# Four graph layers on one core: the block buffers lent to layer 3's first two column pairs, and six small copies moved from GpSimd to ScalarE

## The chip, the core and the metric

The kernel runs on one core of a Trainium2 chip. Its engines are TensorE (matmul; PE in the profile, PEld for its weight loads), VectorE (DVE), ScalarE (ACT), GpSimd (POOL) and SyncE (SP), which here only issues DMAs. The time is that of the device for one execution, in microseconds, from the slowest (here the only) core.

## The reference, cut to what matters

Four layers share one weighted adjacency matrix of 2708 x 2708 and node features of 2708 x 256. Every layer ends in `x = layernorm(x + layer(x))`.

```
# layer 0: adj @ (x * W)
# layer 1: masked attention of four heads, softmax over adj > 0
# layer 2: edge_output = GRU(adj' @ h, h);  edge_support = mean over 3 heads of
#              softmax(leaky(e) where adj' != 0) * adj' @ (h @ W_k)
#          node_output = GRU(edge_support, h)
#          diag(adj) * edge_output + diag(adj) * node_output     (adj' has no diagonal)
# layer 3: z = [x, (adj @ (x @ neigh_W.T)) / (adj.sum(1) + 1)] @ lin_W.T
```

The change lies in layer 2's node GRU and attention and in the start of layer 3's adjacency product.

## The kernel before, in words

The nodes are 22 row tiles of 128 (`NT`), the last with 20 rows. The adjacency comes from the host transposed and cut into 128 x 128 tiles (`adj_t`).

**Products by column pairs.** In layers 2 and 3 the adjacency product is done in seven block products in the place of eight (`seven`, L309): two adjacent column tiles of the matrix, `2c` and `2c+1`, and two row ranges, one from each half of the nodes, make a two by two block. `MH` is 11 such column pairs. VectorE forms sums and differences of the four quarters (L315 to L318), and TensorE does seven products at L328 into four accumulators (`m1`, `m26`, `m75`, `m43`). `gathered` (L332) empties these after the last pair: ScalarE copies `m1`, VectorE combines the rest at L339, L342, L345 and L346.

**Layer 2's attention** is a loop over three row ranges `units` of 512, 512 and 330 rows from each half, three heads `k`, and 11 column pairs `c` (L1336 to L1366). For each pair SyncE loads a block of the adjacency (`load_blocks`, L1147, through `load_pairs`, L259, with its DMAs at L275), and GpSimd clears the diagonal in it (`clear_own`, L278, operation at L286). ScalarE makes a tile `p` of exponentials (L1347, L1350), VectorE multiplies it by the block (L1351), and `seven` follows. The blocks go through three places: two buffers with the tag `blk` in the pool `hold`, and the end of the tile `turn`, in the order block, turn, block. The tiles `p` have three buffers in the pool `nright`. A load into a buffer waits until everything that used the tile before it is done.

**The node cells.** After a row range's heads, its GRU and the rows that follow are a generator, `node` (L1285), which is put into the list `later`; projections of a head go into `urgent` (L300). `between` (L302) takes one step of them; `seven` calls it after chosen products, so that the cells' matmuls stand between those of the next attention range, or of layer 3. Each half of a range goes through `cell` (L1193: gates at L1206, ScalarE at L1208 and L1211, VectorE at L1221 to L1227), then VectorE multiplies by the diagonal and adds the edge part (L1305, L1306), which gives `yt`, the rows transposed. `by_tiles` (L1268) cuts `yt` into the row tiles: a tile that lies whole in the range is used as it stands; of one that is cut by the end of the range, the part is copied into a tile of its own (L1278), and it is used when the second part has come. `node_rows` (L1234) then turns a tile back (TensorE at L1239, through the single PSUM buffer `bank`; ScalarE copies it out at L1241) and takes its moments (VectorE L171 to L175, GpSimd L176); `rows_end` (L1244) multiplies by the layer-3 weights (L1249), and ScalarE writes `h3`, layer 3's right-hand side, in `turn` (L1250), and the rest of the row, which GpSimd stores to memory (L1252). GpSimd also issues the loads for the cells (`load_cell`, L257; `load_diag`, L1265).

Of the row ranges, six partial tiles come from the node cells: two parts in the second half of range 0, two in the second half of range 1, one in each half of range 2. A part has 54 or 74 rows, and the copy moves 2 x 54 or 2 x 74 elements of each partition.

**Layer 3** (L1417 to L1435) has three row ranges `units3` of 430, 430 and 366 rows from each half and again the 11 column pairs, taken in the order `lead`: pairs whose rows of `h3` are ready early come first, so that layer 3 starts while range 2's node cells are still being worked off between its products (`early3`: a step after every product). Each pair is loaded into a tile `p` of `nright`, the same three buffers as in the attention. At the third-last pair of a range a tile `o8` with the tag `blk` is taken, and GpSimd loads into it the stored rows (L1431), which `rows3` (L1402) later adds to. `rows3` uses `by_tiles` as well.

**Order.** Each engine and each queue runs its instructions in a fixed order. It is set before the run by the programming framework, which starts from the order of the code and estimates when each instruction could run; an instruction can so be put ahead of one that stands before it in the code. `issue_after` keeps an instruction behind a named one on its engine: layer 3's pairs but the first are kept behind the end of `gathered` (L1432).

Of the kernel before, what the change touches and what calls it, by code (L numbers as in the profile page):

```python
# [9 lines left out]
F32 = mybir.dt.float32  # L10
# [9 lines left out]
P = 128  # L20
# [7 lines left out]
def kernel(  # L28
# [24 lines left out]
    nc = tc.nc  # L53
    N, F = x.shape
    NT = -(-N // P)
# [6 lines left out]
    W = GT * P  # L62
# [21 lines left out]
    tiles3 = [t for t in range(NT) if t not in last3]  # L84
    NH3 = (N - P * len(last3)) // 2
# [4 lines left out]
    def sz(i):  # L90
        return min(P, N - i * P)

    def width(lo, hi):
        return min(hi * P, N) - lo * P
# [4 lines left out]
    def pieces(lo, w, tiles=range(NT)):  # L99

        for t in tiles:
            a, b = max(lo, 0), min(lo + w, sz(t))
            if a < b:
                yield t, a, b
            lo -= sz(t)
# [5 lines left out]
    def pool(name, bufs=1, **kw):  # L111
        return tc.tile_pool(name=name, bufs=bufs, reuse_waits="tile", **kw)
# [287 lines left out]
    if True:  # L400
# [12 lines left out]
        if True:  # L413
# [39 lines left out]
            with pool("l0", 2) as l0:  # L453
# [49 lines left out]
                with pool("prep", side="right") as prep:  # L503
# [39 lines left out]
                    for f in range(FC):  # L543
                        for s in range(2):
# [7 lines left out]
                            at = s * (H + F)  # L552
# [50 lines left out]
                    t = ahead + 1  # L603
# [35 lines left out]
                t = NT - 1  # L639
# [25 lines left out]
            if True:  # L665
# [124 lines left out]
                for g in range(0, len(spans), 2):  # L790
                    segs = spans[g : g + 2]
                    at, w = segs[0][0] * P, width(segs[0][0], segs[-1][1])
# [20 lines left out]
                    for q in range(H // 2):  # L813
# [23 lines left out]
                        for b, c0 in enumerate(range(0, NT, 2)):  # L837
                            block = {}
                            for c in range(c0, min(c0 + 2, NT)):
                                block[c] = []  # L840
                                for i in range(2):
                                    p = next(held)
# [17 lines left out]
                        got = []  # L860
# [4 lines left out]
                        for s, (p0, ws) in enumerate(cols):  # L865
                            two = slice(2 * (s ^ q) * CT, 2 * ((s ^ q) + 1) * CT)
                            for i, (a, n) in enumerate(halves_at):
                                lo, hi = max(p0, a), min(p0 + ws, a + n)
# [42 lines left out]
                for t in range(NT):  # L911
                    for b, acc in zip(banks, pus):
                        w = width(*spans[b[0]])
                        for j, g in enumerate(b):
                            at = spans[g][0] * P
# [80 lines left out]
                for g in range(0, len(spans), 2):  # L996
                    two, w = range(g, g + 2), width(*spans[g])
                    acc = ps_t.tile([P, 4, P], F32, tag="tr", name="pq").rearrange("p i q -> p (i q)")
                    for t in range(NT):
                        for j, gg in enumerate(two):  # L1000
                            at = spans[gg][0] * P
# [36 lines left out]
                for lo in range(0, NT, 4):  # L1038
                    hi = min(lo + 4, NT)
                    at, w = lo * P, width(lo, hi)  # L1040
                    pt = ps_t.tile([P, 4, P], F32, tag="tr", name="pst")
                    for t in range(lo, hi):
                        n = sz(t)
# [5 lines left out]
                    for u, (a, uw_) in enumerate(units):  # L1049
                        for h in range(2):  # L1050
                            c0, c1 = max(at, h * NH + a), min(at + w, h * NH + a + uw_)
# [52 lines left out]
    hold = hold_stack.enter_context(pool("hold", side="right"))  # L1104
    with pool("e_work") as ework, pool("ps_g", 4, space=PSUM, side="right") as ps_g:
        wih, whh = weights(ework, "wih", e_wih), weights(ework, "whh", e_whh)
        for r, (a, w) in enumerate(raws):
            while len(edges) < min(r + 2, len(raws)):
                next(ahead)
            if r not in left:  # L1110
# [3 lines left out]
                yt = ework.tile([P, FC, 2 * w], F32, tag="yt", name="yt")  # L1114
# [9 lines left out]
    with (  # L1124
# [107 lines left out]
        shared, shared3 = {}, {}  # L1232

        def node_rows(t, src):  # L1234

            n = sz(t)
            pt = bank()
            for f in range(FC):
                nc.tensor.transpose(pt[:n, f * P : (f + 1) * P], src[:, f, :n], ident)  # L1239
            y = nleft.tile([P, F], F32, tag="y", name="y", bufs=3)  # L1240
            nc.scalar.copy(y[:n], pt[:n, :F])  # L1241
            return t, src, y, moments(y, n)[1]

        def rows_end(t, src, y, rs):  # L1244

            n = sz(t)
            pz = bank()
            for f in range(FC):
                nc.tensor.matmul(pz[:n], src[:, f, :n], lwn[:, f, :], start=(f == 0), stop=(f == FC - 1))  # L1249
            nc.scalar.activation(h3[t][:n], pz[:n, F:], AF.Copy, scale=rs)  # L1250
            nc.scalar.activation(y[:n], pz[:n, :F], AF.Copy, scale=rs)
            nc.gpsimd.dma_start(y3_d[t], y[:n])  # L1252

        def load_cell(lo, w):
            got = []
            for parts, tag in ((xt_d, "xt2"), (edge_d.values(), "et")):
                got.append(nleft.tile([P, FC, W], F32, tag=tag, name=tag))
                load_columns(got[-1], parts, lo, w, nc.gpsimd)
            return got

        def load_diag(lo, w):

            dst = nleft.tile([P, W], F32, tag="drow", name="drow")
            src = bass.AP(tensor=diag_d.tensor, offset=diag_d.offset + lo, ap=[[0, P], [1, w]])
            nc.gpsimd.dma_start(dst[:, :w], src)  # L1265
            return dst

        def by_tiles(lo, w, src, ends, among=range(NT)):  # L1268

            tiles, at = [], 0  # L1270
            for t, c0, c1 in pieces(lo, w, among):
                got = src(at, c1 - c0)
                at += c1 - c0
                if c1 - c0 < sz(t):
                    first = t not in ends
                    if first:
                        ends[t] = nleft.tile([P, FC, P], F32, tag=f"yt{len(ends)}", name=f"yt{t}")
                    nc.gpsimd.tensor_copy(ends[t][:, :, c0:c1], got)  # L1278
                    if first:
                        continue  # L1280
                    got = ends[t]
                tiles.append((t, got))
            return tiles

        def node(u, est):  # L1285

            a, w = units[u]
            nxt = None
            for h in range(2):
                lo = h * NH + a  # L1290
                xt, et = nxt or load_cell(lo, w)
                drow = load_diag(lo, w)
                yt = nleft.tile([P, FC, W], F32, tag="yt", name="yt")
                parts = [[a[:, j, :w] for j in range(FC)] for a in (xt, et, yt)]

                def prepare(j):

                    xj, ej, _ = (a[j] for a in parts)
                    nc.vector.tensor_tensor(ej, ej, drow[:, :w], ALU.mult)
                    nc.vector.tensor_tensor(ej, ej, xj, ALU.add)  # L1300

                def rest(j):

                    _, ej, yj = (a[j] for a in parts)
                    nc.vector.tensor_tensor(yj, yj, drow[:, :w], ALU.mult)  # L1305
                    nc.vector.tensor_tensor(yj, yj, ej, ALU.add)  # L1306

                yield from cell(est[h], xt, yt, w, *node_w, b_node, prepare, rest)
                yield
                tiles = by_tiles(lo, w, lambda at, n: yt[:, :, at : at + n], shared)  # L1310
                got = []
                for i in range(len(tiles) + 1):
                    if i < len(tiles):
                        got.append(node_rows(*tiles[i]))
                        yield
                    if i:
                        rows_end(*got[i - 1])
                        yield
                    if i == 1 and h == 0:
                        nxt = load_cell(NH + a, w)  # L1320
# [15 lines left out]
        for u, (_, w) in enumerate(units):  # L1336
            est = [nleft.tile([P, FC, W], F32, tag="est", name="est", bufs=3) for h in range(2)]
            for k in range(K):
                m = accumulators()
                for c in range(MH):  # L1340
                    blk = load_blocks(u, c)
                    pa = nright.tile([P, 2, 2, W], F32, tag="p", name="p", bufs=3)
                    for i in range(2):
                        p = pa[:, i]
                        at = 2 * c + i
# [16 lines left out]
                y, summed = gathered(nleft, m, w, W, "yk")  # L1362
# [6 lines left out]
        def complete(u):  # L1369

            return [t for t in tiles3 if ends3[t] == u]
# [25 lines left out]
        def room():  # L1397

            tag = next(free)
            return bank() if tag is None else ps_a.tile([P, 2, W], F32, tag=tag, name=tag)[:, 0]  # L1400

        def rows3(u, y, o8):  # L1402

            a, w = units3[u]
            for h in range(2):
                for t, src in by_tiles(h * NH3 + a, w, lambda at, n: y[:, :, h, at : at + n], shared3, tiles3):
                    pt = room()
                    for f in range(FC):
                        nc.tensor.transpose(pt[: sz(t), f * P : (f + 1) * P], src[:, f, : sz(t)], ident)
                    row3(t, o8[:, complete(u).index(t)], pt)  # L1410
                    yield
            flush()
# [4 lines left out]
        for u, (_, w) in enumerate(units3):  # L1417
            m = accumulators()
            for i, c in enumerate(lead):
                early3 = u == 0 and max(ends_at[2 * c], ends_at[2 * c + 1]) + 1 < len(units)  # L1420
                if u == 0:
                    if not early3:
                        while urgent or later:
                            between()
                    hq[c] = quarter_sums(xqp, h3, c, "hq")
                pa = nright.tile([P, 2, 2, W], F32, tag="p", name="p", bufs=3)
                load_pairs(units3, u, c, pa, NH3, tiles3)
                if i == MH - 3:
                    o8 = hold.tile([P, 4 * W // F, F], F32, tag="blk", name="o8", bufs=2)
                    for j, t in enumerate(complete(u)):  # L1430
                        nc.gpsimd.dma_start(o8[: sz(t), j], y3_d[t])  # L1431
                with tc.issue_after(summed.ins) if i else nullcontext():  # L1432
                    seven(nright, m, pa, h3, hq[c], c, w, i == 0, i == MH - 1, range(7) if early3 else (2, 5))
            y, summed = gathered(nleft, m, w, W, "yk")
            later.append(rows3(u, y, o8))  # L1435
# [287 lines left out]
```

## Time and profile before

| | |
|---|---|
| median of 3 runs | 1851.02 us (1850.7 to 1851.26) |
| the profiled execution's own time | 1851.49 us |
| its span, first to last instruction | 1849.7 us |
| mean granted TensorE clock | 0.996 |
| TensorE busy | 1822.9 us (99%) |
| VectorE busy | 1267.4 us (69%) |
| ScalarE busy | 698.7 us (38%) |
| GpSimd busy | 297.1 us (16%) |
| attention and node cells, about | 725 to 1600 us |
| layer 3, about | 1600 us to the end |

The profile is one execution. In its views, each line of a timeline gives start and length in us, the engine, the line of the kernel, the operation, what is written and read, how many instructions, and in brackets the idle time before them with what ended it. A tile is named with what it was allocated as; `m` are the accumulators, `bank` the single buffer of the cells, `hq` and `turn` layer 3's right-hand sides and sums of them, `xq` and `x` those of layer 2. One float product at L328 shows as two matmul records. A busy share of TensorE is not its speed: the granted clock beside it says how fast it ran.

### The profile page before, as it was taken

The numbers are of one execution on the slowest core, as the hardware profiler recorded it, in microseconds if no ns is written. First come the engines' busy times: TensorE is split into PE (matmuls) and PEld (weight loads), VectorE is DVE, ScalarE is ACT, GpSimd is POOL, SyncE is SP. The second block draws the span as 40 slices with busy tenths as digits, with TensorE's granted clock in tenths as the row PEclk, the third lists the DMA queues.
The fourth block names the chain that finished last, engine by engine and source line by source line (L and its number), as shares of the span: only waits on it lengthen the run. The fifth ranks groups of instructions, "written<-read, shape, count | busy, mean of one in ns | idle before, by whom it ended". The sixth has DMA issues, their size and how long they took to land.

```text
span 1849.7 us, 23045 instructions
## 1 busy us (share of the span) xinstructions
PE 1822.9 (99%) x7512; PEld 1039.6 (56%) x7512; DVE 1267.4 (69%) x2242; ACT 698.7 (38%) x1443; POOL 297.1 (16%) x447
## 2 busy tenths in 40 slices
PE   9999999999999999999999999999999999999997
PEld 7888843233456886887444444444445556554555
DVE  5333489998797655654658887777887767844664
ACT  3444420033245113111555665555664655321011
POOL 1332211011013410000011101211200302111211
PEclk9999999999999999999999999999999999999999
DMA  9343310000003657764557665454554545634774
GB/s 301 122 161 125 126 55 24 24 1 27 27 7 89 145 143 193 175 144 117 171 145 203 179 174 153 132 158 121 164 153 112 144 103 131 170 89 120 205 175 125
DMA packets 435711, 237.34 MB, mean 128 GB/s; under 512 B 184459, under 2 KB 422444, under 8 KB 433148
## 3 DMA queue, kind: packets, MB, share of 16 engines
q1 hardware_dynamic: 423534, 210.76, 42.1%
q0 software_dynamic: 7696, 20.50, 3.5%
q10 hardware_dynamic: 4350, 4.50, 0.7%
q8 instruction: 62, 1.02, 0.2%
q14 instruction: 69, 0.57, 0.1%
HBM read 223.00 MB, written 12.66 MB: 127 GB/s over the span
## 4 chain that ended last, share of the span: by engine, by line
PE 92%; DMA 3%; DVE 2%; SPq 1%; ACT 1%; issue 1%; POOL 0%; POOLq 0%; DVEq 0%
PE m L328 43%; PE acc L820 11%; PE acc L214 8%; PE bank L1206 7%; PE den L830 6%; PE gate L1081 4%; PE bank L1182 3%; PE bank L1249 2%; PE acc L519 2%; SPq L275 1%; PE pm L425 1%; PE m L1450 1%; DMA strip<-in_adj_t_dram 1%; PE pq L1002 1%; ACT below L472 1%
## 5 line engine op out<-in xcount | busy, mean ns | idle before, releaser
L844 DVE SCALAR_TENSOR_TENSOR p<-fall_b,rise,mask 128x1024 f32<-128x1024 f32 (+1 forms) x264 | 288.7, 1158 | 28.8 <-PE den L830 17.8
L1347 ACT ACTIVATE p<-st,e_neg 128x1024 f32<-128x1024 f32 (+1 forms) x198 | 197.6, 1042 | 195.1 <-PE m L328 190.0
L328 PE MATMUL m<-s,xq 128*128 128x512 f32 (+3 forms) x660 | 230.7, 468 | 0.0
L820 PE MATMUL acc<-p,h 128*64 128x512 f32 (+2 forms) x1056 | 210.5, 549 | 0.0
L315 DVE TENSOR_TENSOR s<-p 128x512 f32<-128x512 f32 (+3 forms) x132 | 81.9, 620 | 153.0 <-PE m L328 106.2
L328 PE MATMUL m<-p,xq 128*128 128x512 f32 (+1 forms) x396 | 183.5, 545 | 0.1
L214 PE MATMUL acc<-turn,strip 128*128 128x257 f32 x792 | 182.6, 381 | 0.3 <-DMA strip<-in_adj_t_dram 0.2
L1350 ACT ACTIVATE p<-p 128x1024 f32<-128x1024 f32 (+1 forms) x198 | 179.0, 944 | 0.2
L328 PE MATMUL m<-p,x 128*128 128x512 f32 (+1 forms) x396 | 167.6, 542 | 0.3 <-DVE supt L345 0.3
L328 PEld LDWEIGHTS m<-s,xq 128*128 128x128 f32 x660 | 124.7, 190 | 76.1 <-issue 59.0
L1351 DVE TENSOR_TENSOR p<-p,blk 128x1024 f32<-128x1024 f32 (+1 forms) x132 | 143.6, 1108 | 34.5 <-ACT p L1350 25.1
L214 PEld LDWEIGHTS acc<-turn,strip 128*128 128x128 f32 x792 | 147.2, 189 | 22.0 <-DMA strip<-in_adj_t_dram 1.4
L820 PEld LDWEIGHTS acc<-p,h 128*64 128x64 f32 x1056 | 72.7, 138 | 129.7 <-issue 122.2
L328 PE MATMUL m<-s,x 128*128 128x512 f32 (+3 forms) x330 | 127.2, 467 | 0.0
L328 PEld LDWEIGHTS m<-p,xq 128*128 128x128 f32 x396 | 74.9, 191 | 77.2 <-issue 61.9
L328 PEld LDWEIGHTS m<-p,x 128*128 128x128 f32 x396 | 74.8, 190 | 75.5 <-issue 60.9
L457 DVE TENSOR_SCALAR mask<-strip 128x2816 fp8e4<-128x2816 f32 (+5 forms) x40 | 39.3, 1012 | 109.2 <-DMA strip<-in_adj_t_dram 109.2
L830 PE MATMUL den<-p,h 128*32 128x512 f32 (+2 forms) x1056 | 110.5, 546 | 0.0
L286 POOL TENSOR_TENSOR blk<-blk,offdiag 128x128 f32<-128x128 f32 (+3 forms) x50 | 33.8, 681 | 365.4 <-DMA blk<-in_adj_t_dram 312.2
L472 ACT ACTIVATE below<-strip 128x384 bf16<-128x384 f32 x132 | 78.6, 595 | 18.3 <-DMA strip<-in_adj_t_dram 14.8
L328 PEld LDWEIGHTS m<-s,x 128*128 128x128 f32 x330 | 62.2, 191 | 39.0 <-issue 34.8
L316 DVE TENSOR_TENSOR p<-p 128x512 f32<-128x512 f32 (+3 forms) x132 | 81.6, 618 | 2.4
(286 smaller groups left out, 2652.6 us busy)
## 6 DMA issues: line engine op xcount, KB each, us to landing
strip<-in_adj_t_dram SPq DMA_DIRECT2D x19, 1408.0 KB, 6.0
blk<-in_adj_t_dram SPq DMA_DIRECT2D x88, 256.0 KB, 3.5
blk<-in_adj_t_dram SPq DMA_DIRECT2D x88, 192.0 KB, 4.1
pa<-in_adj_t_dram SPq DMA_DIRECT2D x110, 128.0 KB, 2.7
turn<-in_adj_t_dram SPq DMA_DIRECT2D x44, 256.0 KB, 3.1
blk<-in_adj_t_dram SPq DMA_DIRECT2D x88, 128.0 KB, 2.6
p<-in_adj_t_dram SPq DMA_DIRECT2D x88, 128.0 KB, 2.8
turn<-in_adj_t_dram SPq DMA_DIRECT2D x44, 192.0 KB, 3.2
```

The lines of the kernel that those rows point to most:

```text
L214: at = nc.tensor.matmul(acc, s[:, c, :n], rhs(c), start=(c == 0), stop=(c == NT - 1))
L315: nc.vector.tensor_tensor(s1, a21, a22, ALU.add)
L316: nc.vector.tensor_tensor(a21, a21, a11, ALU.subtract)
L328: nc.tensor.matmul(dst[:, :w], lt, rt, start=start and not (one_bank and i in (3, 4, 6)), stop=stop and not (one_bank and i in (1, 2, 5)))
L472: nc.scalar.activation(below[:, : (hi - lo) * P], s[:, lo:hi].rearrange("p c n -> p (c n)"), AF.Relu, scale=-1.0, accum_out=negative[:, BE ...
L820: at = nc.tensor.matmul(acc[s][i * HD : (i + 1) * HD, :ws], hs[c][:, 2 * q + i, :HD], ps[i][:, p0 : p0 + ws], **flags,)
L830: at = nc.tensor.matmul(den[j : j + CT, :ws], hs[c][:, 2 * q + i, HD + 1 - CT :], ps[i][:, p0 : p0 + ws], **flags,)
L844: nc.vector.scalar_tensor_tensor(p[:, :w], fall_b[:, i, :w], rise[:, c, 2 * q + i : 2 * q + i + 1], mask[:, c, at : at + w], ALU.max, ALU. ...
L1206: nc.tensor.matmul(g[:, :w], lt, rt, start=(q == 0), stop=(q == len(terms) - 1))
L1347: nc.scalar.activation(p[:, :, :w], st_k[:, :, :w], AF.Relu, scale=-1.0, bias=e_neg[:, at, k : k + 1])
L1350: nc.scalar.activation(p[:, :, :w], p[:, :, :w], AF.Exp, scale=-1.0)
L1351: nc.vector.tensor_tensor(p[:, :, :w], p[:, :, :w], blk[:, i, :, :w], ALU.mult)
```

## The change

It has two parts that don't depend on each other.

`by_tiles` takes the copying instruction as a parameter. The node cells pass ScalarE's copy, layer 3's `rows3` passes GpSimd's, which it was for both. In layer 3, for the first row range's first two pairs, the tile is taken from the two `blk` buffers of `hold`, under the name `p3`, and not from the three `p` buffers of `nright`; the third pair is then the first in a `p` buffer. The size of these tiles is the same, so the memory in use stays what it was. `o8` takes the same two buffers after them.

```diff
-        def by_tiles(lo, w, src, ends, among=range(NT)):
+        def by_tiles(lo, w, src, ends, copy, among=range(NT)):
...
-                    nc.gpsimd.tensor_copy(ends[t][:, :, c0:c1], got)
+                    copy(ends[t][:, :, c0:c1], got)
...
-                tiles = by_tiles(lo, w, lambda at, n: yt[:, :, at : at + n], shared)
+                tiles = by_tiles(lo, w, lambda at, n: yt[:, :, at : at + n], shared, nc.scalar.copy)
...
-                for t, src in by_tiles(h * NH3 + a, w, lambda at, n: y[:, :, h, at : at + n], shared3, tiles3):
+                for t, src in by_tiles(h * NH3 + a, w, lambda at, n: y[:, :, h, at : at + n], shared3, nc.gpsimd.tensor_copy, tiles3):
...
-                pa = nright.tile([P, 2, 2, W], F32, tag="p", name="p", bufs=3)
+                if u == 0 and i < 2:
+                    pa = hold.tile([P, 2, 2, W], F32, tag="blk", name="p3", bufs=2)
+                else:
+                    pa = nright.tile([P, 2, 2, W], F32, tag="p", name="p", bufs=3)
                 load_pairs(units3, u, c, pa, NH3, tiles3)
                 if i == MH - 3:
                     o8 = hold.tile([P, 4 * W // F, F], F32, tag="blk", name="o8", bufs=2)
```

## The prediction

> **What bounds the kernel now.** First the page's chain of work that ended last:
>
> ```profile
> PE 92%; DMA 3%; DVE 2%; SPq 1%; ACT 1%; issue 1%; POOL 0%; POOLq 0%; DVEq 0%
> ```
>
> TensorE is the chain, so only a stretch in which TensorE stands still, or runs slowly, can be won. The waits of TensorE alone, from 1200 us to the end (the last third, where the change lies; columns: total, times, longest), name them:
>
> ```profile
> PE m L328 <- DVE yk L339: 2.6, 1, 2.6
> PE bank L1239 <- POOL yt L1278: 2.5, 2, 2.2
> PE bank L1409 <- POOL yt L1278: 0.2, 1, 0.2
> ```
>
> That is all: two real stalls in 650 us. One is at L1278, the copy that moves to ScalarE; the other is where layer 3 begins. The windows show what each costs beyond its idle time (columns: stretch, length, PE, PEld, DVE, ACT and POOL busy, granted clock, DMA share, GB/s):
>
> ```profile
> 1526.00:1534.00 8.00, 5.78 (x18) 3.66 (x17) 4.73 (x11) 3.36 (x7) 4.48 (x8) 0.79 0.39 100
> 1552.00:1600.00 48.00, 48.00 (x174) 32.47 (x174) 46.11 (x102) 28.09 (x41) 9.89 (x19) 1.00 0.57 143
> 1600.00:1606.00 6.00, 4.46 (x16) 2.62 (x14) 1.45 (x3) 0.44 (x1) 0.53 (x1) 1.00 1.11 299
> 1606.00:1612.50 6.50, 5.41 (x11) 2.63 (x12) 6.36 (x11) 0.00 (x0) 0.00 (x0) 0.74 0.61 149
> ```
>
> Between the stalls TensorE is full at clock 1.00; just after each the clock is 0.79 and 0.74.
>
> Stall A, in order of time, GpSimd first, then TensorE:
>
> ```profile
> 1527.22 1.48 POOL L286 TENSOR_TENSOR blk<-blk,offdiag 128x128 f32<-128x128 f32 x2 [4.84 <-DMA blk<-in_adj_t_dram]
> 1528.65 0.58 POOL L1265 DMA_DIRECT2D drow<-diag_d  x1
> 1529.24 0.53 POOL L1278 COPY yt<-yt 128x108 f32<-128x108 f32 x2
> ...
> 1529.57 0.69 PE L1239 MATMUL bank<-ident,yt 128*128 128x128 f32 x2 [2.22 <-POOL yt L1278]
> 1530.06 1.31 PE L328 MATMUL m<-s,xq 128*128 128x330 f32 x2
> ```
>
> The copy's input was ready at 1526.83 (VectorE's L1306: 1526.14 + 0.69). The copy ran at 1529.24 because GpSimd's queue held the diagonal clearing of an adjacency block (L286), which waited 4.84 us for its load, and a load of the diagonal (L1265). All engines then stood: VectorE waited 2.08 us at L171, ScalarE 2.81 at L1241.
>
> Stall B, SyncE's queue, VectorE, TensorE:
>
> ```profile
> 1586.38 2.00 SPq L275 DMA_DIRECT2D blk<-in_adj_t_dram  x4
> 1595.44 4.79 SPq L275 DMA_DIRECT2D p<-in_adj_t_dram  x9
> ...
> 1604.52 0.61 DVE L315 TENSOR_TENSOR s<-p 128x430 f32<-128x430 f32 x1 [5.47 <-DMA p<-in_adj_t_dram]
> ...
> 1606.20 0.84 DVE L339 TENSOR_TENSOR yk<-m1s,m 128x660 f32<-128x660 f32 x1
> ...
> 1607.09 0.99 PE L328 MATMUL m<-p,turn 128*128 128x430 f32 x2 [2.63 <-DVE yk L339]
> ```
>
> SyncE had nothing to do from 1588.38 to 1595.44: layer 3's first pair needs a "p" buffer, free only when TensorE has read the third-last attention block. Its seven loads land near 1604.3. VectorE holds that pair's L315 to L317 ahead of L339, which empties the accumulators of the attention; TensorE's second product of layer 3 wants those accumulators. So a late load stops TensorE through VectorE's order.
>
> **What the Trainium skill says.** "TensorE: Matmul & The Clock Gate", section "What's actually happening": after about 3.4 us of idleness the array runs at half clock and needs about as long a busy time to return. The trace agrees in kind: idle 2.22 and 2.63 us, then two products of 330 columns take 1.31 us instead of 0.72. The same page, "Architectural detail": ScalarE's, VectorE's and GpSimd's queues are strictly in order; L1278 standing behind L286 agrees. "ScalarE: Activation LUTs", "What ACT_TABLE_LOAD costs": 186 ns + 0.833 ns an element without pointer operands, so an estimated 276 ns for 108 elements and 309 for 148. The trace's nearest row, L336 copying 226 elements, takes 349 ns (formula: 374), so it holds to 7%. "DMA: Bandwidth & Descriptors", "Issuing engines are not separate DMA queues": loads issued by GpSimd and by SyncE share the 16 engines. Agrees: with eleven "o" loads of 128 KB from GpSimd between 1588.6 and 1600, the first pair's loads saw a DMA share of 1.11 and its seventh took 5.8 us to land (all L275 loads: median 2.8).
>
> **The change, part by part.**
>
> *Copies.* Six leave GpSimd (616 and 809 ns at 1289, 281 and 312 at 1529, 373 at 1643.8, 276 at 1678.5: 2.7 us) and come to ScalarE as 3 x 276 + 3 x 309 ns = 1.8 us, hidden under ScalarE's waits for TensorE (1.89 us before L1347 at 1288 and again at 1294; 2.69 before 1644.0; 3.02 before 1679.3). Uncovered they would cost 1.8 us. On GpSimd nothing is lost.
>
> At 1529: ScalarE ends its L1350 pair at 1527.49, then waits until 1530.30. The copy cannot stand behind ScalarE's next L1347 (1532.50): that one waits for products that TensorE has queued behind the transposes. So it runs at 1527.5 to 1527.8, the transposes at 1527.8 instead of 1529.57. Then, at full clock: 4 transposes at 0.11, products of 330 columns at 0.277 each; VectorE's L171 can follow L1351 at 1528.63 instead of 1530.70, so L1351's second half ends near 1530.3 instead of 1532.36. TensorE reaches "m<-p,x" at about 1530.4 instead of 1533.41: 3.0 us by TensorE, 2.1 by VectorE's shift alone. I take 2.8, since VectorE had 1.19 us of slack at its next L315. Queued behind the copy on ScalarE are L1241 (wanted later) and L1347; a copy that waits for yt could hold L1347. At 1289 the worst order (copies ahead of the L1347 of 1288.01) makes the exponentials 1.6 us late against 0.7 us of slack before TensorE's 1295.12: at most about 1 us. I charge 0.4. The copy of 1678.5 had TensorE waiting 0.23 us; ScalarE is idle there: no change.
>
> *First two pairs.* The block buffer of the third-last attention block is free when VectorE's L1351 has multiplied it (1586.49 + 1.59 = 1588.1), the other one at 1594.87 + 1.60 = 1596.5. So pair 0 issues from 1588.4 (SyncE done with the last block), seven issues at 0.5 us to 1592, landed by about 1596, 7 us earlier; pair 1 from 1596.5 instead of 1599.3. Pairs 2, 3, 4 get the three "p" buffers without waiting for pair 0. VectorE's L315 then waits for the "s" buffer, free when TensorE ends the second-last block (1599.7), and L317 ends near 1601.6, ahead of L339. L339 waits for its accumulators (1602.6) and ends at 1603.5; L345 ends near 1604.7, L346 at 1605.6, L1364 at 1607.2.
>
> TensorE: layer 3's first product starts at 1603.57 as before, the second (needs L339) at 1604.29, the third (needs L345) at 1605.0: no wait. Before, it took from 1603.57 to 1612.50 for six pairs of products. Full speed is 19.68 us / 54 = 0.364 each (chain, 1694.19), so 12 x 0.364 = 4.4 us; the loss is 8.93 - 4.4 = 4.5. The projection that follows at 1612.5 needs L1364, before 1611.82, now 1607.2, in time for 1607.9. Gain 4.5; at least 2.6 (the idle alone), at most 4.9.
>
> *The eleven "o" loads* (L1431) use those same two buffers at 1588.6 and 1596.8; now they wait until layer 3 has used pairs 0 and 1, about 1609 and 1617. GpSimd sits idle there from 1600.5 to 1640.35, and the rows that read them come at 1715: hidden, and off pair 0's transfers. If GpSimd's order put them in front of L257 at 1640, they are still issued 20 us earlier.
>
> Sum: 2.8 + 4.5 - 0.4 = 6.9 us. The profiled span 1849.7 becomes 1842.8; its execution took 1851.49, 1.8 around the span. From the median of 1851.02: 1844.1. After both places TensorE is full (18.00 of 18.00 us in 1534 to 1552), and loads hang on its progress, so the gain should reach the end.
>
> **Rivals.**
> (1) Only the loads help: the copy is placed on ScalarE behind something late, or the stall moves to another producer. For: VectorE's own shift is smaller. Against: ScalarE's 2.81 us of idleness. 1851.0 - 4.5 = 1846.5.
> (2) The loads do not come earlier (SyncE's order keeps them behind, or VectorE takes L315 late anyway), the copy helps: 1848.2. Against: 7.06 us of empty SyncE queue. With the copies failing too, no change: 1851.
> (3) Slower: the interleave is lost. From 1612 to 1694 each gate, projection and row product goes through one PSUM bank, and its emptying (0.56 to 0.60 us of weight-load idleness at each group) is covered by one layer-3 product put between. With pairs loaded early, the order fixed ahead of the run can put layer-3 products before their turn and leave the groups back to back. 4 projections, 16 gates and some 8 row groups, 28 x 0.6 = 17 us; all exposed: 1851 - 7 + 17 = 1861. It decides from 12 exposed groups (break-even), 19 for slower by 0.2%. For: VectorE's L315 standing before L339 shows that the order is not the code's. Against: the number of products between is the same.
>
> **How the numbers follow.** Both gains 0.66; (1) 0.12; (2) and no change 0.08; (3) 0.14. Within 0.2% (3.7 us, about what a measurement can tell) is only (2): faster 0.78, same 0.08, slower 0.14. The likeliest: 1844. Its own bounds: 7.9 us won (3.0 + 4.9) is 1843, with half a microsecond for noise 1842.5; 4.7 won is 1846.3. Cases (1) and (2) stretch the upper end to 1848.5.
>
> **What would show it.** Right: no TensorE wait on GpSimd near 1527, clock 1.00 there; "p3" loads from about 1585 (all is 3 us earlier), no wait at L339, clock 1.00 through the start of layer 3, "o" loads some 20 us later. Wrong: TensorE waiting for ScalarE at L1239, a new wait at L1182 or L1206, idle TensorE between 1605 and 1690, or VectorE waiting for "s" with an attention block queued behind it.

## The result and the profile after

The changed kernel took 1844.3 us (median of 6 runs, 1841.32 to 1846.04), the kernel before 1851.14 beside it: a ratio of 0.9962, 95% interval 0.9951 to 0.9973. By the ratio that is about 7.0 us. The forecast was 1844.0 and faster. The profiled execution had a span of 1843.5 us, 6.2 less than before. Two more sets of runs, shown below, gave 0.9970 and 0.9964. The kernel before itself took between 1846.9 and 1851.3 in the four sets, so times are compared as ratios within a set only.

The page's chain by engine, and TensorE's waits from 1200 us on (total, times, longest):

```profile
PE 91%; DMA 3%; DVE 2%; ACT 1%; SPq 1%; issue 1%; POOL 0%; POOLq 0%; DVEq 0%
...
PE m L328 <- DVE p L316: 1.0, 2, 0.7
PE bank L1409 <- POOL yt L1278: 0.2, 1, 0.2
```

The waits at L339 and L1239 are gone. A smaller one at L316 is new, late in layer 3. The windows at the two places (columns: stretch, length, PE, PEld, DVE, ACT and POOL busy, granted clock, DMA share, GB/s) are full, at clock 1.00; before, it was 0.79 around the first stall and 0.74 just behind the second:

```profile
1526.00:1534.00 8.00, 8.00 (x30) 5.02 (x29) 7.95 (x19) 6.84 (x12) 3.98 (x7) 1.00 0.56 138
1597.00:1612.00 15.00, 15.00 (x48) 8.51 (x47) 13.32 (x23) 0.43 (x1) 2.18 (x4) 1.00 0.82 227
```

Stall A after the change, in timelines of GpSimd, ScalarE and TensorE:

```profile
1527.89 0.98 POOL L286 TENSOR_TENSOR blk<-blk,offdiag 128x128 f32<-128x128 f32 x2 [4.17 <-DMA blk<-in_adj_t_dram]
...
1528.20 0.50 ACT L1278 COPY yt<-yt 128x108 f32<-128x108 f32 x2
...
1528.54 0.44 PE L1239 MATMUL bank<-ident,yt 128*128 128x128 f32 x2
1528.81 0.72 PE L328 MATMUL m<-s,xq 128*128 128x330 f32 x2
```

GpSimd still waits 4.17 us for the block's load before it clears the diagonal, but the copy no longer stands behind it: its input is ready at 1528.16 (L1306: 1527.48 + 0.68), and it starts at 1528.20, between ScalarE's exponentials.

Stall B, in timelines of SyncE, VectorE, TensorE and GpSimd:

```profile
1585.80 21.82 SPq L275 DMA_DIRECT2D p<-in_adj_t_dram  x35
...
1597.15 0.61 DVE L315 TENSOR_TENSOR s<-p 128x430 f32<-128x430 f32 x1 [0.79 <-PE m L328]
...
1600.00 0.84 DVE L339 TENSOR_TENSOR yk<-m1s,m 128x660 f32<-128x660 f32 x1 [0.44 <-PE m L328]
...
1600.84 1.61 PE L328 MATMUL m<-p,turn 128*128 128x430 f32 x4
1602.31 0.99 PE L328 MATMUL m<-p,hq 128*128 128x430 f32 x2
...
1606.61 2.18 POOL L1434 DMA_DIRECT2D o<-y  x4 [17.63 <-DMA p<-in_adj_t_dram]
```

The first pair's loads start at 1585.80, 15 us before TensorE comes to it (before: 8 us). VectorE's L315 waits for TensorE to leave the "s" buffer, no longer for a load. TensorE does layer 3's first products back to back, and GpSimd's first "o" loads come only at 1606.61.

The same events in both traces give the account. First the lines of TensorE that it starts and ends with at each stall, before and then after (layer 3's first product after the change is shown above):

```profile
1526.63 0.72 PE L328 MATMUL m<-s,xq 128*128 128x330 f32 x2
1533.41 1.27 PE L328 MATMUL m<-p,x 128*128 128x330 f32 x4
1603.57 0.89 PE L328 MATMUL m<-p,turn 128*128 128x430 f32 x2
1613.61 0.89 PE L328 MATMUL m<-s,turn 128*128 128x430 f32 x2
```

```profile
1527.97 0.72 PE L328 MATMUL m<-s,xq 128*128 128x330 f32 x2
1530.70 1.27 PE L328 MATMUL m<-p,x 128*128 128x330 f32 x4
1606.46 0.89 PE L328 MATMUL m<-s,turn 128*128 128x430 f32 x2
```

Then all of them (us from the start of each span):

| event on TensorE | before | after | difference |
|---|---|---|---|
| last product ahead of the transposes (L328, "s,xq") | 1526.63 | 1527.97 | +1.34 |
| first "p,x" behind the transposes | 1533.41 | 1530.70 | -2.71 |
| layer 3's first product | 1603.57 | 1600.84 | -2.73 |
| first pair's last product ("s,turn") | 1613.61 | 1606.46 | -7.15 |
| last row product of the cells (L1249, 20 rows) | 1692.29 | 1685.41 | -6.88 |
| products of the last two row tiles (L1450; after: L1453) | 1818.80 | 1812.58 | -6.22 |

This execution came to the change 1.34 us late, among other things for 1.5 us more of waits for strips in layer 0, which no line of the change touches. Stall A then gave 4.05 us and stall B 4.42; 0.93 went again in the rest of layer 3.

### The profile page after: what moved, and what is told of

It reads as the page before. It is cut to its first block, busy times and chain, and to the rows that moved or that the text cites. A ratio compares the mean times of both kernels' runs of the same rounds, so it can differ in the third digit from the quotient of the medians.

```text
span 1843.5 us, 23048 instructions
## 1 busy us (share of the span) xinstructions
PE 1819.7 (99%) x7512; PEld 1038.2 (56%) x7512; DVE 1267.9 (69%) x2242; ACT 699.0 (38%) x1449; POOL 287.3 (16%) x441
## 4 chain that ended last, share of the span: by engine, by line
PE 91%; DMA 3%; DVE 2%; ACT 1%; SPq 1%; issue 1%; POOL 0%; POOLq 0%; DVEq 0%
PE m L328 42%; PE acc L820 11%; PE acc L214 8%; PE bank L1206 8%; PE den L830 6%; PE gate L1081 4%; PE bank L1182 3%; PE bank L1249 2%; PE acc L519 2%; PE pm L425 1%; DMA strip<-in_adj_t_dram 1%; SPq L275 1%; PE m L1453 1%; DMA p<-in_adj_t_dram 1%; PE pq L1002 1%
## 5 line engine op out<-in xcount | busy, mean ns | idle before, releaser
L328 PE MATMUL m<-s,xq 128*128 128x512 f32 (+3 forms) x660 | 230.1, 467 | 0.0
L328 PE MATMUL m<-p,xq 128*128 128x512 f32 (+1 forms) x396 | 183.0, 544 | 0.2
L315 DVE TENSOR_TENSOR s<-p 128x512 f32<-128x512 f32 (+3 forms) x132 | 82.1, 622 | 146.8 <-PE m L328 115.1
L1350 ACT ACTIVATE p<-p 128x1024 f32<-128x1024 f32 (+1 forms) x198 | 179.0, 943 | 0.2
L328 PE MATMUL m<-p,x 128*128 128x512 f32 (+1 forms) x396 | 167.6, 542 | 0.3 <-DVE supt L345 0.3
L328 PEld LDWEIGHTS m<-s,xq 128*128 128x128 f32 x660 | 124.5, 190 | 76.1 <-issue 59.5
L1351 DVE TENSOR_TENSOR p<-p,blk 128x1024 f32<-128x1024 f32 (+1 forms) x132 | 142.9, 1102 | 34.4 <-ACT p L1350 23.4
L328 PE MATMUL m<-s,x 128*128 128x512 f32 (+3 forms) x330 | 127.0, 467 | 0.0
L328 PEld LDWEIGHTS m<-p,xq 128*128 128x128 f32 x396 | 74.6, 190 | 76.9 <-issue 61.0
L328 PEld LDWEIGHTS m<-p,x 128*128 128x128 f32 x396 | 74.8, 190 | 75.5 <-issue 60.9
L286 POOL TENSOR_TENSOR blk<-blk,offdiag 128x128 f32<-128x128 f32 (+3 forms) x50 | 29.1, 588 | 375.2 <-DMA blk<-in_adj_t_dram 326.3
L328 PEld LDWEIGHTS m<-s,x 128*128 128x128 f32 x330 | 62.0, 190 | 39.0 <-issue 34.6
L316 DVE TENSOR_TENSOR p<-p 128x512 f32<-128x512 f32 (+3 forms) x132 | 81.9, 620 | 2.4
```

Source lines behind the costliest of these rows:

```text
L315: nc.vector.tensor_tensor(s1, a21, a22, ALU.add)
L316: nc.vector.tensor_tensor(a21, a21, a11, ALU.subtract)
L328: nc.tensor.matmul(dst[:, :w], lt, rt, start=start and not (one_bank and i in (3, 4, 6)), stop=stop and not (one_bank and i in (1, 2, 5)))
L1350: nc.scalar.activation(p[:, :, :w], p[:, :, :w], AF.Exp, scale=-1.0)
L1351: nc.vector.tensor_tensor(p[:, :, :w], p[:, :, :w], blk[:, i, :, :w], ALU.mult)
```

## The experiments

All times are medians in us; ratios are to the kernel before in the same set of runs, with the 95% interval.

### Each part alone

The copies on ScalarE alone, and the first two pairs' tiles alone; the diffs are the two halves of the change.

> The copies alone, on ScalarE. Theory (stall A is the copy waiting in GpSimd's order behind a block's load, and its end is worth the whole of what the trace shows between 1526.6 and 1533.4): 4.0 us faster than the kernel before, TensorE without a wait at L1239 and clock 1.00 from 1526 to 1534; stall B as it was (a wait at L339 of about 2.6 us). Prediction's sizing: 2.8 us minus 0.4. Rival (the gain comes from the loads, the copy's wait is passed on to another producer): within 1 us of before.

Measured: 1844.23 against 1847.36, ratio 0.9986 (0.9980 to 0.9993), so 2.6 us.

> The first two pairs' loads alone; copies stay on GpSimd. Theory: 4.4 us faster than before, no wait at L339, layer 3's start at clock 1.00, stall A as it was (2.2 us idle at L1239 near 1527). Some of it, up to 1 us, may be given back in layer 3's later ranges. If the two parts add up, the two single gains sum to that of the whole change, about 7 us. Rival (lost interleave of cells and layer 3): no gain, TensorE idle between 1612 and 1694.

Measured: 1844.52, ratio 0.9984 (0.9978 to 0.9991), so 3.0 us. No interleave was lost: from 1612 to 1694 TensorE was busy for 81.8 of 82 us.

Each part removes its own stall and leaves the other. Each is worth less than the 4.0 and 4.4 us expected from the account above, and the stall that is left, with the window around it, shows why. First loads_two, which keeps stall A:

```profile
1528.07 0.44 PE L1239 MATMUL bank<-ident,yt 128*128 128x128 f32 x2 [1.56 <-POOL yt L1278]
1525.00:1533.00 8.00, 6.44 (x25) 4.03 (x24) 6.90 (x17) 5.27 (x9) 5.42 (x9) 1.00 0.44 115
```

Then copies_scalar, which keeps stall B:

```profile
1597.44 0.99 PE L328 MATMUL m<-p,turn 128*128 128x430 f32 x2 [1.49 <-DVE yk L339]
1594.00:1603.00 9.00, 7.42 (x22) 3.54 (x21) 7.96 (x13) 0.00 (x0) 0.00 (x0) 1.00 0.87 217
```

Here TensorE's idleness was 1.56 and 1.49 us, against 2.22 and 2.63 in the one trace of the kernel before, and the clock stayed at 1.00. Measured like the account above, against the whole change's first trace, these stalls cost 1.7 us (4.44 between the two events instead of 2.73) and 2.2 us (7.82 instead of 5.62). The longer ones were followed by products at about half speed and cost 4.05 and 4.42. So a part's gain depends on how long that stall is in the execution, and whether the clock falls after it. The trace on which the prediction rests shows the long end: in four later traces of kernels that leave the copy on GpSimd, stall A was 1.48 to 1.56 us.

### The whole change again

> The whole change once more, beside single parts measured against the same runs of the kernel before. If the parts add up: the sum of the two single gains found so far, 0.14% and 0.16%, so a ratio near 0.9970. If the first measurement (0.9962) holds on any chip: 0.9962. The difference would come from the clock: where a stall is short enough not to bring a slow clock after it, its removal is worth its idle time alone (1.6 us at L1239, 1.5 to 2.7 at L339).

Measured: 1842.2 against 1846.91, ratio 0.9970 (0.9958 to 0.9982). That is 5.5 us. The two single ratios multiplied give 0.9970: within the intervals, the parts add up. A third set gave 0.9964:

> The whole change, as the yardstick of the three others of this call: 0.9965 to 0.9972 of the kernel before.

Measured: 1844.78 against 1851.29, ratio 0.9964 (0.9953 to 0.9976), so 6.7 us. The wait at L316 was 0.3 us in the first of these two traces and absent in the second: the 1.0 us of the first profile is not a fixed part of the change.

### The copies on VectorE

```diff
-                    nc.gpsimd.tensor_copy(ends[t][:, :, c0:c1], got)
+                    copy(ends[t][:, :, c0:c1], got)
...
+                tiles = by_tiles(lo, w, lambda at, n: yt[:, :, at : at + n], shared, nc.vector.tensor_copy)
```

> The copies alone, but on VectorE instead of ScalarE. Theory (what counts is only that they leave GpSimd's queue, where the diagonal clearing waits for a load): as good as on ScalarE to within 1 us, so about 3 to 4 us faster than before; VectorE has them right behind L1306, which makes their input. Rival (ScalarE's idleness is what makes it work; VectorE's order is too full): less than 1.5 us faster, with waits of TensorE on VectorE near 1527.

Measured: 1845.75, ratio 0.9993 (0.9985 to 1.0001): 1.3 us, in an interval that takes in no gain. It is well short of the 3 to 4 us of the theory; the rival's gain of less than 1.5 us and its wait on VectorE came, the wait a short one. TensorE's wait at the transposes:

```profile
1524.08 0.41 PE L1239 MATMUL bank<-ident,yt 128*128 128x128 f32 x2 [0.38 <-DVE yt L1278]
```

The stall shrinks to 0.38 us here and is gone on ScalarE: on both queues tried in place of GpSimd's, the copy no longer waits for the block's load. That GpSimd's order was the cause of stall A stands. VectorE's copy is placed behind L316, and from there on VectorE's operations come in another order. Whether the 1.3 us by which this fell behind ScalarE's version is more than chance, the two intervals, which overlap, don't settle. The traces show where they differ: stall B, which both versions keep, was 2.72 us here, followed by a slow clock (0.89 from 1597 to 1612), and 1.49 us at clock 1.00 in copies_scalar. Whether VectorE's order or the execution made it longer is open.

### One pair in the place of two

```diff
-                if u == 0 and i < 2:
+                if u == 0 and i < 1:
```

(against the tiles alone; the copies are on GpSimd)

> Only the first pair's tile from the block buffers, copies on GpSimd. Theory: the second pair's load was never late enough (in the kernel before it is issued from 1599.3 and VectorE turns to it at 1609.7), so one pair does all: the same as two pairs, ratio near 0.9984, no wait at L339. Rival (the second pair's earlier load counts, because VectorE is ready for it some 6 us earlier now): about half of it, with VectorE waiting for a load between 1600 and 1606.

Measured: 1844.07 against 1846.91, ratio 0.9981 (0.9971 to 0.9991); with two pairs, in another set, it was 0.9984. No wait at L339, none of VectorE for the second pair. One pair does it.

### Is it the late buffer, or the collision of transfers?

In the kernel before, the last seven of GpSimd's eleven loads of the stored rows are issued just when the first pair's loads are (from 1595.44 on):

```profile
1596.76 3.77 POOL L1431 DMA_DIRECT2D o<-y  x7 [4.34 <-DVE hq L294]
```

Here the pairs keep their buffers, and only the loads of the stored rows go later:

```diff
-            nc.gpsimd.dma_start(dst[:, :w], src)
+            diag_loads.append(nc.gpsimd.dma_start(dst[:, :w], src))
...
-                    for j, t in enumerate(complete(u)):
-                        nc.gpsimd.dma_start(o8[: sz(t), j], y3_d[t])
+                    with tc.issue_after(diag_loads[-1].ins):
+                        for j, t in enumerate(complete(u)):
+                            nc.gpsimd.dma_start(o8[: sz(t), j], y3_d[t])
```

> The kernel before, with one change: GpSimd's loads of the stored rows for layer 3's first ranges (eleven of 128 KB, which the kernel before issues between 1588 and 1600) are kept behind the last node cell's load of the diagonal, some 45 us later. The pairs keep their three buffers. Theory of the prediction (the buffer comes free too late): the first pair still issues only from 1595.4; it lands at best 2.8 us after its last issue at 1598.9, so at 1601.7 instead of 1604.3, and stall B shrinks but doesn't go: 1 to 2 us faster. Rival (the collision of transfers is the whole cause, the buffer's time isn't): landing at 1601.7 is early enough, L339 ends near 1604.4, just when TensorE wants it, and 4 us or more are won without lending any buffer.

Measured: 1843.33 against 1847.36, ratio 0.9985 (0.9976 to 0.9993), 2.8 us: as much as lending the buffers (0.9984), more than the 1 to 2 us of the prediction's theory and less than the 4 of the rival. SyncE, VectorE and TensorE in its trace:

```profile
1589.43 16.61 SPq L275 DMA_DIRECT2D p<-in_adj_t_dram  x28
...
1595.72 0.61 DVE L315 TENSOR_TENSOR s<-p 128x430 f32<-128x430 f32 x1 [2.83 <-DMA p<-in_adj_t_dram]
...
1597.40 0.83 DVE L339 TENSOR_TENSOR yk<-m1s,m 128x660 f32<-128x660 f32 x1
...
1597.56 1.73 PE L328 MATMUL m<-p,turn 128*128 128x430 f32 x4
```

From the first issue to VectorE's L315 it is 6.3 us (1589.43 to 1595.72); it was 9.1 before (1595.44 to 1604.52). The buffer is as late as ever, VectorE still waits 2.83 us for the load, and TensorE no longer waits at L339: its two products run on with 0.1 us lost. The collision took 2.8 us between these two traces, and those were what made a late load into a stall.

Seven traces agree. In each the first issue comes 8.1 us before TensorE's first product of layer 3. With the "o" loads beside the pair's it is 9.08, 9.17 and 7.94 us from the first issue to L315 (before, copies_vector, copies_scalar), and TensorE waits 2.63, 2.72 and 1.49 us at L339: each time 6.45 less. With those loads later it is 5.7 to 6.3 us (this run and the next three below), and TensorE waits there for 0.1 us at most.

Lending the buffers starts the load earlier and also takes the "o" loads out of its way, since they need the same two buffers. No run starts the load earlier and leaves the "o" loads beside it, so what the earlier start is worth alone isn't shown.

With the copies on ScalarE as well:

> Copies on ScalarE and the eleven loads of stored rows kept back, without any block buffer lent. If the collision of transfers was the cause of stall B, this equals the whole change to within 1 us (ratio near 0.997); if the buffer's time counts by itself, it falls behind by the 0.1 us of wait and the half-bank steps seen when the loads alone were kept back, still within 1 us. Against it: GpSimd issues the kept-back loads between the powers of the last node cell, which may hold TensorE at L1249.

Measured: 1840.06 against 1846.91, ratio 0.9966 (0.9955 to 0.9976), beside 0.9970 of the whole change. Again, with the whole change at 0.9964 beside it:

> Copies on ScalarE, stored rows loaded later, no buffer lent, once more. If keeping the transfers apart does all that lending does: within 0.1% of the whole change. If its first 0.9966 against 0.9970 was more than chance: faster than the whole change by 0.1%.

Measured: 1844.43 against 1851.29, ratio 0.9968 (0.9957 to 0.9978). Within the intervals the same as the whole change, without a block buffer lent. The first of the two traces shows what it pays for standing between GpSimd's other work (a wait of TensorE):

```profile
PE bank L1206 <- ACT y L1251: 0.7, 1, 0.7
```

### Can the loads go later still, and do both measures add up?

The stored rows' loads behind the last store of the cells (in place of the last load of the diagonal), first without and then with the buffers lent.

> As before, but the stored rows' loads kept behind the last node cell's last store, so that none stands between GpSimd's powers (TensorE waited 0.7 us at L1206 for L1251 where they did). Expected: that wait gone, up to 1 us faster than with the loads at the earlier place. Against it: the eleven loads then fall, 6 us of issuing, into the stretch where layer 3's second range is loaded, 20 us before they are read.

Measured: 1846.59 against 1851.29, ratio 0.9977 (0.9966 to 0.9988).

> The whole change with the stored rows' loads also kept behind the last node cell's last store. Since both measures remove the same stall, nothing is won on top: equal to the whole change to within 0.1%. If lending and keeping apart added up, it would be 3 us faster than the whole change.

Measured: 1847.03, ratio 0.9975 (0.9966 to 0.9985). Nothing adds up, and the later place looks worse, in both versions by about 0.1%. In scalar_o_last the wait at L1206 went, but the 1 us expected from that did not come. In both_o_last, TensorE's waits from 1500 us on begin with:

```profile
PE m L328 <- DVE yk L339: 1.3, 1, 1.3
PE m L328 <- DVE p L316: 0.7, 1, 0.7
PE m L328 <- DVE yk L345: 0.6, 1, 0.6
```

L339 and L345 are the emptying of the accumulators once more, now at the end of layer 3's first row range (1707): the same kind of stall in another place. GpSimd issues the "o" loads from 1690.2 to 1697.4, beside the loads of the next range, and VectorE again waits 3.68 us for a load in front of L339. No version here beats the whole change by more than the measurement is uncertain.

### VectorE's order

```diff
-                with tc.issue_after(summed.ins) if i else nullcontext():
+                with tc.issue_after(summed.ins):
```

> The kernel before, but VectorE's operations of layer 3's first pair are kept behind the end of the emptying of the accumulators (L346), as those of the other pairs already are. Nothing is loaded earlier. Theory (a late load stops TensorE only through VectorE's order): no wait of TensorE at L339; it waits instead, up to 1.8 us, for the first pair's L316, since that load is as late as before; 1 to 3 us faster. Rival (the load's lateness decides, whatever the order): no faster. Since the order of layer 3's products changes with it, the interleave could also be lost: then slower, with TensorE idle at L1182 or L1206.

Measured: 1847.79 against 1846.91, ratio 1.0005 (0.9997 to 1.0013): no gain. TensorE's waits from 1200 us on, its first three lines:

```profile
PE m L328 <- DMA p<-in_adj_t_dram: 2.8, 2, 1.4
PE bank L1239 <- POOL yt L1278: 1.7, 2, 1.5
PE m L328 <- DVE yk L346: 0.8, 1, 0.8
```

The wait at L339 went and came back as two waits of TensorE for the load itself, since its second product reads the pair as loaded. The rival was right here: whatever VectorE's order, the data were late. (TensorE's order of layer 3's products changed too, so this run isn't of VectorE's order alone.)

## Why the prediction was right, point by point

- **Where the time was.** Two stalls, both of which went; the rest of TensorE's work stayed as it was. Right, and each part alone takes away its own.
- **Stall A, 2.8 us (2.1 to 3.0).** Right in kind, too small for that trace: 4.05. Two steps failed. The copy was put behind both of ScalarE's L1350, with the transposes some 0.6 us later than TensorE could take them; it stands between the two, right behind its input, and TensorE doesn't wait. And VectorE's order was kept, with L171 holding up L318 and L1351, for some 0.5 us more; in the changed kernel L318 stands ahead of L171 (1529.91 and 1530.33). TensorE went from 1527.97 to 1530.70 without a gap. Where the clock didn't fall, the same stall cost 1.7 us; the single part measured 2.6.
- **ScalarE's cost, 0.4 us at 1289.** Not found. The two copies took 0.49 us there, between exponentials, and TensorE didn't wait. The estimates of 276 and 309 ns, from the formula in the Trainium skill's "ScalarE: Activation LUTs", "What ACT_TABLE_LOAD costs", hold: all six took 277 to 317.
- **Stall B, 4.5 us (2.6 to 4.9).** 4.42 in that trace; 3.0 for the single part, from medians. How long the stall was in the kernel before in that set isn't on record; in the two traces that keep it, it was 1.49 and 2.72.
- **Its cause.** Half right. That the load is late, and that VectorE's order passes this on, is in the trace, and lending one buffer cures it. But the prediction took the time at which the buffer comes free for the cause, and the "o" loads for a side remark, and it counted all eleven of them beside the first pair's, where seven were. The runs show that a late buffer alone is not enough: with those loads elsewhere, a buffer just as late does no harm. And the way through VectorE is not the only one: with it closed, TensorE waits for the load.
- **"The gain should reach the end."** 7.15 of lead at layer 3's first pair, 6.22 at its last rows; in the two later traces TensorE waited 0.3 us and not at all where the first lost 1.0.
- **The rivals.** Both single ones fell with the parts' own gains. The lost interleave didn't come: from 1612 to 1694 TensorE was busy for 82.0 of 82 us.
- **The sum.** 6.9 us forecast; by the ratios 7.0 measured first, 5.5 and 6.7 in the later sets. The close hit of the first is partly luck: a stall sized too small and a cost that didn't come on one side, the 0.9 us given back, which wasn't forecast, on the other, cancel in part. And both stalls were sized from one trace, in which they were long.

## What to carry to other kernels

Look at what stands in the same in-order queue ahead of a small operation on the critical path: a copy of 0.3 us cost up to 4 because the operation before it waited for a load. Where a load is late at a change of stage, ask first which other transfers run beside it; moving loads that nobody needs for 100 us can be worth as much as a buffer. And size a stall as a range, from more than one trace if there is one: here it cost its idleness and 0.2 or 0.7 us where the clock held, its idleness and 1.6 to 1.9 us where it fell.

## What the runs showed of the hardware that was not expected

The fall of TensorE's granted clock after a short stall isn't fixed. The change of layers near 560 us, long before anything that was edited, has one gap of 1.55 us or 1.56 in each of the fourteen traces. From 555 to 575 us the clock was 0.91 in eight of them and 1.00 in six. Two are of the same kernel, the whole change, from its first and its third set:

```profile
555.00:575.00 20.00, 18.45 (x150) 9.20 (x148) 14.73 (x24) 5.70 (x18) 5.25 (x6) 0.91 0.09 27
```

```profile
555.00:575.00 20.00, 18.45 (x164) 9.38 (x162) 16.19 (x28) 5.70 (x18) 5.26 (x6) 1.00 0.09 27
```

At equal busy time, the first lost some 1.6 us: the 56 products behind the gap took 8.51 us in it and 6.93 in the second. The Trainium skill ("TensorE: Matmul & The Clock Gate", "What's actually happening") describes a free-running window of about 3.4 us; that its position decides here would fit, but no run tests it. Against the 3.4 us of idleness that the prediction took from that page, gaps of 2.22, 2.63 and 2.72 us (the last in copies_vector) were each followed by a slow clock here. Gaps of about 1.5 us may or may not be: near 560 us they were in eight of fourteen traces, at stalls A and B in none of the five traces that have one so short. Where the clock fell, the loss beyond the idleness was much the same each time, whatever the gap: 1.8 us at both stalls of the kernel before, 1.9 in copies_vector, 1.6 near 560 us. Executions of one kernel can so differ by some 1.6 us at such a place, more than half of what one part of this change is worth.
